# A GroupNorm, attention and 7x7 convolution kernel: edge rows stored once per column phase and read at offsets, constants kept in buffers, one block of v begun earlier

## The chip, the core and the metric

The kernel runs on one core of a Trainium2 chip, in one launch. The core has a matrix engine (TensorE, in the profile PE, its weight loads PEld), three engines for element-wise work (VectorE or DVE, ScalarE or ACT, GpSimd or POOL) and a queue that only issues transfers (SyncE, SP). Transfers between the chip's memory (HBM, tensors in a pool called `dram` here) and the on-chip buffers are issued by SP, ACT or POOL and carried by 16 DMA engines that all of them share. The metric is the device time of one execution in microseconds, lower is better.

## What is computed

Everything is float32. Two layers follow each other on an image `x` of 384 channels, 192 x 192:

```python
def layer0(x):                            # x: (1, 384, 192, 192)
    qkv = einsum('bchw,oc->bohw', x, w_qkv) + b_qkv           # 1152 channels
    qkv = qkv.reshape(b, 3*c, 96, 2, 96, 2).max(axis=(3, 5))  # 2x2 max pooling
    qkv = depthwise_conv3x3(qkv, w_dw) + b_dw
    q, k, v = split(qkv, 3)                                   # 8 heads of 48 channels
    q, k = q / norm(q), k / norm(k)                           # over the 9216 places
    attn = einsum('bhcn,bhdn->bhcd', q, k) * temperature      # 48 x 48 per head
    out = sum(topk_softmax(attn, kk) @ v * a for kk, a in ((24, a1), (32, a2), (36, a3), (38, a4)))
    out = repeat2x2(gelu(out))
    return einsum('bchw,oc->bohw', out, w_proj) + b_proj

def layer1(x):                            # depthwise 7x7, padding 3
    w_sym = (w + rot90(w, 1) + rot90(w, 2) + rot90(w, 3)) * 0.25
    return depthwise_conv7x7(x, w_sym)

x = x + layer0(groupnorm(x))              # 32 groups
x = x + layer1(groupnorm(x))
```

## The kernel before

Five stages follow each other.

**Statistics (0 to 130 us).** `x` is read once for the first GroupNorm.

**q and k (130 to 1330 us).** 24 blocks of eight image rows: TensorE multiplies (`pooled`, L662), VectorE pools and runs the 3x3 taps (`depthwise`, L717), transposes feed the products q times k in `grams`. Beside it, POOL builds the weights of the 7x7 convolution: `weights` (L571) writes banded weight rows into a tile `g` and stores them to two tensors in HBM, `wt` (inner rows) and `wh` (edge rows). SP stores a few constant rows from the tile `z` into `wh` and `sh` (L620 to L631).

**Attention's matrix (1330 to 1440 us).** `attention` (L881) is a generator: each `next` puts some of its steps into the program, and between them stand multiplications for v. It ends with a matrix `diag` filled by ten small transfers (L983), transposed on TensorE into `aT` (L990) and copied to `attnT`.

**v, projection, residual (1440 to 2190 us).** The image's rows are dealt into 16 blocks of two rows of each of six row bands of 32 (TR = 32, NT = 6, RB = 2), in the order 13, 14, 15, 0, 1, and so on. For each block i (L1217) `load_v` fills a third of the buffer `xvs` from SP's queue, `convolve` multiplies and pools, `depthwise_v` runs the taps, `attend` and `project` follow for block i - 2, and `residual` (L1142) adds the image rows `xr` (three buffers, loaded by SP, L1139) and stores the result for the last stage. Instructions marked `keep` stay in the written order on their engine.

`residual` writes a tile `sx` (three buffers in turn). The image's columns are split into four phases (CP = 4): column 4j + p is element j of phase p. A row of `sd` is one phase of one row in all six bands, RUN = 6 x 50 elements. Every block's two rows go to `sd` by POOL (L1197). The convolution of a band also needs three rows above and three below it. The first and the last three rows of the bands (block rows 0 to 2 and 29 to 31, that is blocks 14, 15, 0 and 1) are stored a second time, as edge rows, to `sh`, shifted by one band. Ten column shifts are wanted (NQ = CP + 7 - 1 = 10), so each edge row is stored three times, with four, four and two shifts (L1204 to L1210).

**The 7x7 convolution (2190 to 2775 us).** 48 steps of eight channels (CB = 8). The 128 partitions hold 4 phases x 32 rows. A step multiplies three weight tiles with three data tiles: two column offsets of `main` and one tile `aux` with all that `main` lacks. In `aux`, partitions 0 to 31 and 96 to 127 are copied from `main`; partitions 32 to 95 are read from `sh`: 30 upper edge rows, a row of ones (it carries the bias), a zero row, 30 lower edge rows, two zero rows. Loads run two steps ahead into three buffers each (`w`, `h`, `main`, `aux`), the first two steps' from SP, the others from ACT's queue (L1304). Per step, POOL runs `borders` for the next step (L1462): it adds the channel's mean, through masks in `mm`, to the padding columns of `main` and `aux`, and writes it by a copy into the padding rows of `aux`, so that padding becomes zero after the second GroupNorm. POOL also rearranges the result (`spread`, L1521), and SP stores it. VectorE puts 1/rstd into the middle of the weights (`middle`, L1405). The lines that read the edge rows:

```python
def load_aux(n):
    aux = auxs[n % len(auxs)]
    queue(n)(aux.rearrange("p c t j -> p c (t j)")[TOP:REST], sh[:, span(n)])
    return aux
```

Of the kernel before, what the change touches and what calls it, by code (L numbers as in the profile page):

```python
# [13 lines left out]
P = 128  # L14
# [55 lines left out]

TOP = 32
BOT = 64
ONE = TOP + HALO * NQ
# [13 lines left out]
def conv_preact_d2(  # L87
# [29 lines left out]
    sh = dram.tile([SHR, C, RUN], F32, name="sh")  # L117
# [445 lines left out]
    with ExitStack() as bx:  # L563
# [6 lines left out]
        def weights(kt, i0, i1):  # L570

            g = gwp.tile([P, GR, GQ, TR], F32, name=f"g{kt}_{i0}", tag="g")
            nc.gpsimd.memset(g, 0.0)
            for kr in range(KS):
                lo, hi = max(i0, kr), min(i1, kr + TR)  # L580
                if lo < hi:
                    nc.gpsimd.tensor_copy(
                        bass.AP(
                            g.tensor,
                            g.offset + ((lo - i0) * GQ + CP - 1) * TR + lo - kr,
                            [g.ap[0], [TR, KS], [GQ * TR + 1, hi - lo]],
                        ),
                        w7s[:, kt, kr, :].unsqueeze(2).to_broadcast([P, KS, hi - lo]),
                    )
            lo, hi = max(i0, HALO), min(i1, HALO + TR)  # L590
            cs = slice(kt * P, (kt + 1) * P)
            for v in range(CP if lo < hi else 0):
                nc.gpsimd.dma_start(
                    wt[v * TR + lo - HALO : v * TR + hi - HALO, cs].rearrange("f c n -> c f n"),
                    bass.AP(
                        g.tensor,
                        g.offset + ((lo - i0) * GQ + v) * TR,
                        [g.ap[0], [GQ * TR, hi - lo], [1, 2 * P]],
                    ),
                )  # L600
            for i in range(i0, i1):
                if HALO <= i < HALO + TR:
                    continue
                f = i * NQ if i < HALO else BOT - TOP + (i - HALO - TR) * NQ
                nc.gpsimd.dma_start(
                    wh[f : f + NQ, cs].rearrange("f c n -> c f n"),
                    bass.AP(
                        g.tensor,
                        g.offset + (i - i0) * GQ * TR,
                        [g.ap[0], [TR, NQ], [1, P]],  # L610
                    ),
                )
# [6 lines left out]
        with tc.issue_after(loaded):  # L619
            for kt in range(KT):  # L620
                cs = slice(kt * P, (kt + 1) * P)
                for f in (ONE, BOT + HALO * NQ):
                    nc.sync.dma_start(
                        wh[f - TOP : f - TOP + 2, cs].rearrange("f c n -> c f n"),
                        z[:, RUN : RUN + 2 * P].rearrange("p (f n) -> p f n", f=2),
                    )
                    for k in range(2):
                        one = f + k == ONE
                        nc.sync.dma_start(
                            sh[f + k - TOP, cs], z[:, 0:RUN] if one else z[:, RUN : 2 * RUN]  # L630
                        )  # L631
# [249 lines left out]
    def attention(ap):  # L881
# [102 lines left out]
        yield  # L984
        for dt in range(KT):
# [3 lines left out]
            for ct in range(lo // P, (hi - 1) // P + 1):  # L989
                nc.tensor.transpose(  # L990
                    ps[:, ct * P : (ct + 1) * P], diag[:, ct, dt * P : (dt + 1) * P], ident
                )
# [57 lines left out]
    with tc.tile_pool(name="ap", bufs=1) as ap:  # L1050
        chain = attention(ap)
        for _ in range(9):
            next(chain, None)
        i = AHEAD - 1
        for t0 in range(0, NT, UT):
            xb = load_v(i, t0)
            with tc.issue_after(multiplied):
                for ct in range(KT):
                    convolve(i, t0, ct, xb, lambda ins: ins)
            for _ in range(6):  # L1060
                next(chain, None)
        for ct in range(KT):
            depthwise_v(1, ct, (0, 1))
        for _ in chain:
            pass
# [76 lines left out]
    def residual(i, ot, y, xr, pin):  # L1142
# [52 lines left out]
        for a in range(RB):  # L1195
# [3 lines left out]
            halos = []  # L1199
            if r >= TR - HALO:  # L1200
                halos.append(((r - TR + HALO) * NQ, -JP))
            if r < HALO:
                halos.append((BOT - TOP + r * NQ, JP))
            for h, shift in halos:  # L1204
                for q in range(0, NQ, CP):
                    nv = min(CP, NQ - q)
                    nc.gpsimd.dma_start(
                        sh[h + q : h + q + nv, cs].rearrange("f c n -> c f n"),
                        rows_of(a, nv, shift + q // CP),
# [7 lines left out]
    for i in range(AHEAD, NBC):  # L1217
        j = i - 2
        xb = load_v(i, 0)
        for ct in range(KT):  # L1220
# [58 lines left out]
    with ExitStack() as ex_:  # L1279
# [57 lines left out]
        def load_aux(n):  # L1337
            aux = auxs[n % len(auxs)]
            queue(n)(aux.rearrange("p c t j -> p c (t j)")[TOP:REST], sh[:, span(n)])
            return aux  # L1340

# [3 lines left out]
        for n in range(2):  # L1345
            ws[n] = ws[n] if n == 0 else load_w(n), hs[n]
# [4 lines left out]
        mask = wide.tile([P, 5], F32, name="mask")  # L1351
# [4 lines left out]
        part = wide.tile([P, 4], F32, name="part")  # L1356
        for k, (base, q) in enumerate(((TOP, 0), (BOT, 0), (TOP, NQ - HALO), (BOT, NQ - HALO))):
            hits = ident[:, base : base + HALO * NQ].rearrange("p (h q) -> p h q", q=NQ)
            nc.vector.tensor_reduce(
                part[:, k : k + 1], hits[:, :, q : q + HALO], AX.XY, ALU.add  # L1360
            )
        nc.vector.tensor_tensor(mask[:, 3:4], part[:, 0:1], part[:, 1:2], ALU.add)
        nc.vector.tensor_tensor(mask[:, 4:5], part[:, 2:3], part[:, 3:4], ALU.add)
# [30 lines left out]
        mm = wide.tile([P, C, 5], F32, name="mm")  # L1394
# [30 lines left out]
        def masked(kt):  # L1425
            keep(
                nc.vector.tensor_tensor(
                    mm[:, tiled(kt), :],
                    mb[:, tiled(kt)].unsqueeze(2).to_broadcast([P, P, 5]),
                    mask.unsqueeze(1).to_broadcast([P, P, 5]),  # L1430
# [9 lines left out]
        masked(0)  # L1440
# [3 lines left out]
        middle(0)  # L1444
        sumw = const.tile([P, KT], F32, name="sumw")
# [14 lines left out]
        nc.sync.dma_start(wh[ONE - TOP].rearrange("(t p) n -> p t n", p=P), offs)  # L1460

        def borders(n):  # L1462
# [24 lines left out]
            for base, t in ((TOP, 0), (BOT, NT - 1)):  # L1487
                ends = aux[base : base + TOP, :, :, 0 : NJ : NJ - 1]
                keep(
                    nc.gpsimd.tensor_tensor(  # L1490
                        ends, ends,
                        mm[base : base + TOP, cs, 3:5].unsqueeze(2).to_broadcast([TOP, CB, NT, 2]),
                        ALU.add,
                    )
                )
                keep(
                    nc.gpsimd.tensor_copy(  # L1497
                        aux[base : base + HALO * NQ, :, t, 0:NJ],
                        mb[base : base + HALO * NQ, cs].unsqueeze(2).to_broadcast(
                            [HALO * NQ, CB, NJ]  # L1500
                        ),
                    )
                )
# [154 lines left out]
```

## Time and profile before

| what | us |
|---|---|
| median of 3 runs | 2758.66 |
| lowest and highest of them | 2756.45, 2759.91 |
| the profiled execution, whole | 2777.17 |
| its span in the profile | 2775.5 |
| TensorE busy in it | 2584.4 |
| VectorE busy | 2449.2 |
| ScalarE busy | 1141.4 |
| GpSimd busy | 744.6 |

The span is the time from the first to the last instruction of the one execution that was profiled. Busy times add up the instructions of an engine. Strips of 40 digits show the busy share of an engine in 40 equal slices of the span (69.4 us each), in tenths; PEclk is the clock granted to TensorE. In the lines on groups and waits, "L549 PE MATMUL pv<-xv,wq" is line 549, its engine and operation, the tile written and those read; "<-" at the end of a line names what an engine waited for. The share of DMA is the mean over 16 engines.

### The profile page before, as it was taken

The page shows a single profiled execution, that of the slowest core. Times are in us where ns is not written, and L with a number is a line of the kernel's source. Part 1 is how long each engine was busy: PE and PEld are TensorE (multiplying, and loading weights), DVE is VectorE, ACT ScalarE, POOL GpSimd, SP SyncE. Part 2 cuts the span into 40 slices and gives each one's busy share as a digit, 9 for nine tenths or more (in the row PEclk, how much of TensorE's full clock was granted, in tenths as well). Part 3 has the DMA queues.
Part 4 walks back from the last instruction along what each step waited for, and adds up shares of the span by engine and source line. Part 5 has one row for each costly group of instructions (what it writes and reads, how often), then busy time and mean ns, then how long its engine had stood idle before and what let it go on. Part 6 is the DMA issues. An engine that isn't in the chain of part 4 may idle for free. (4 is left out here: it accounts for less than half of the span.)

```text
span 2775.5 us, 25750 instructions
## 1 busy us (share of the span) xinstructions
PE 2584.4 (93%) x8365; PEld 1525.9 (55%) x8365; DVE 2449.2 (88%) x3538; ACT 1141.4 (41%) x2262; POOL 744.6 (27%) x885
## 2 busy tenths in 40 slices
PE   0399999999999999999979969999999899999998
PEld 0144444444444444444646646666666677777776
DVE  7989999999999999999889859989889788888887
ACT  0143333343433343443302212222324577777776
POOL 1024444100000000000011321010101578877876
PEclk9999999999999999999999989999999899999999
DMA  9976667311010101112227997575665899999998
GB/s 379 402 257 216 231 221 251 121 53 50 35 68 35 68 35 45 58 34 68 83 90 248 350 331 247 174 253 201 221 223 172 330 343 364 370 372 371 365 376 260
DMA packets 234087, 581.01 MB, mean 209 GB/s; under 512 B 16688, under 2 KB 165792, under 8 KB 217184
## 3 DMA queue, kind: packets, MB, share of 16 engines
q1 hardware_dynamic: 173456, 283.44, 29.2%
q0 software_dynamic: 37376, 148.85, 15.9%
q10 hardware_dynamic: 23120, 147.07, 14.1%
q8 instruction: 67, 1.10, 0.2%
q14 instruction: 68, 0.56, 0.1%
HBM read 370.93 MB, written 208.21 MB: 209 GB/s over the span
## 5 line engine op out<-in xcount | busy, mean ns | idle before, releaser
L662 PE MATMUL pq<-xq,wq 128*128 128x512 f32 x2268 | 1021.9, 595 | 0.0
L717 DVE SCALAR_TENSOR_TENSOR qk<-ring,wd,qk 128x384 f32<-128x384 f32 x1152 | 696.3, 615 | 25.0
L662 PEld LDWEIGHTS pq<-xq,wq 128*128 128x128 f32 x2268 | 411.7, 190 | 421.9 <-issue 371.4
L549 PE MATMUL pv<-xv,wq 128*128 128x384 f32 x1512 | 500.3, 491 | 29.2 <-DMA xv<-in_x_dram 23.9
L1562 PE MATMUL pc<-main,w 128*128 128x288 f32 x1536 | 435.2, 406 | 3.7 <-POOL aux L1497 1.1
L549 PEld LDWEIGHTS pv<-xv,wq 128*128 128x128 f32 x1512 | 289.1, 192 | 231.5 <-issue 22.6
L1582 DVE TENSOR_SCALAR apart<-pc,rb 32x576 f32<-32x576 f32 x384 | 312.2, 813 | 75.6 <-PE pc L1562 59.4
L1562 PEld LDWEIGHTS pc<-main,w 128*128 128x128 f32 x1536 | 289.3, 189 | 88.4 <-issue 3.4
L672 DVE TENSOR_REDUCE ring<-pq 128x128 f32<-128x512 f32 x428 | 290.0, 679 | 52.2 <-PE pq L662 51.4
L1580 ACT ACTIVATE apart<-pc,rb 32x576 f32<-32x576 f32 x384 | 281.4, 733 | 132.3 <-PE pc L1562 127.5
L735 ACT COPY qkT<-turns 32x288 f32<-32x288 f32 x768 | 329.5, 429 | 12.0 <-DVE turns L781 3.2
L1039 DVE SCALAR_TENSOR_TENSOR vb<-rows,wd,vb 128x576 f32<-128x576 f32 x384 | 313.2, 817 | 11.1
L729 ACT ACTIVATE junk<-qk 128x384 f32<-128x384 f32 x144 | 71.2, 494 | 471.9 <-DVE qk L717 471.1
L1562 PE MATMUL pc<-aux,h 128*128 128x288 f32 x768 | 248.5, 405 | 0.3 <-issue 0.3
L803 POOL TENSOR_TENSOR rn<-rn,halfpos 128x6 f32<-128x6 f32 x1 | 1.4, 1362 | 842.8 <-DVE rn L802 842.8
L1521 POOL COPY res<-apart 128x1152 f32<-128x1152 f32 (+1 forms) x96 | 223.4, 2353 | 10.8 <-ACT apart L1580 7.3
L1156 DVE TENSOR_TENSOR sx<-xr,y 128x576 f32<-128x576 f32 x180 | 203.8, 1174 | 24.0 <-ACT y L1127 14.9
L1197 POOL DMA_DIRECT2D sd<-sx x96 | 72.4, 757 | 517.2 <-DVE sx L1156 496.2
L555 DVE TENSOR_REDUCE rows<-pv 128x192 f32<-128x768 f32 x144 | 137.6, 956 | 71.8 <-PE pv L549 71.8
L1405 DVE SCALAR_TENSOR_TENSOR w<-eye,sb,w 128x512 f32<-128x512 f32 x96 | 171.9, 1830 | 1.5
L1176 ACT ACTIVATE wq<-sx,negmid 128x1152 f32<-128x1152 f32 x96 | 120.6, 1257 | 125.3 <-DVE sx L1156 121.2
L1562 PEld LDWEIGHTS pc<-aux,h 128*128 128x128 f32 x768 | 144.7, 189 | 42.8 <-POOL main L1470 1.9
(234 smaller groups left out, 2252.3 us busy)
## 6 DMA issues: line engine op xcount, KB each, us to landing
sd<-sx POOLq DMA_DIRECT2D x96, 600.0 KB, 10.3
out_dram<-res SPq DMA_DIRECT2D x192, 288.0 KB, 11.0
main<-sd ACTq DMA_DIRECT2D x46, 1200.0 KB, 6.9
xr<-in_x_dram SPq DMA_DIRECT2D x45, 1152.0 KB, 12.8
xq<-in_x_dram SPq DMA_DIRECT2D x21, 2304.0 KB, 7.9
xv<-in_x_dram SPq DMA_DIRECT2D x126, 384.0 KB, 7.0
w<-wt ACTq DMA_DIRECT2D x46, 1024.0 KB, 6.9
xs<-in_x_dram SPq DMA_DIRECT2D x24, 1536.0 KB, 15.1
```

Of the source, the lines that this page charges most:

```text
L549: nc.tensor.matmul(ps[:, u, 0 : RB * HW], wq[:, kt, o : o + P], xb[:, u, kt, :], start=(kt == 0), stop=(kt == KT - 1),)
L662: ins = nc.tensor.matmul(ps, wq[:, kt, ct * P : (ct + 1) * P], rows[:, kt, :, g * 64 : (g + 1) * 64], start=(kt == 0), stop=(kt == KT - 1) ...
L672: ins = nc.vector.tensor_reduce(t[:, r0 : r0 + PR, 1 + g * 32 : 1 + (g + 1) * 32], ps.rearrange("p (h a w b) -> p h w a b", h=PR, a=2, b=2 ...
L717: pin(nc.vector.scalar_tensor_tensor(dst, src, w, dst, ALU.mult, ALU.add))
L735: nc.scalar.copy(side[f * Q : (f + 1) * Q].rearrange("p c (t n) -> p t c n", n=P)[:, :, :, a * Q : (a + 1) * Q], turns[a * Q : (a + 1) * Q ...
L1039: pin(nc.vector.scalar_tensor_tensor(dst, src, w, dst, ALU.mult, ALU.add))
L1156: nc.vector.tensor_tensor(bass.AP(flat.tensor, flat.offset + at(e) + a * RUN, [flat.ap[0], [JP, NT], [1, NJ], [at(f) - at(e), 2]],), xq[:, ...
L1405: nc.vector.scalar_tensor_tensor(mid, eye.unsqueeze(1).to_broadcast([P, 4, P]), sb[:, c : c + 1], mid, ALU.mult, ALU.add,)
L1521: keep(copy(res[ps, k], apart[ps, :, k].rearrange("p e n -> p n e")))
L1562: nc.tensor.matmul(ahead[q][:, k, 0 : NT * NJ], lhs, rhs, start=(j == 0), stop=(j == 2), skip_group_check=True,)
L1580: keep(nc.scalar.mul(dst, src, scale))
L1582: keep(nc.vector.tensor_scalar_mul(dst, src, scale))
```

## The change

Edge rows. `sh` gets 24 rows (EDGE = 2 x 3 x 4: above and below, three rows, four phases) and one zero row. `residual` stores each edge row once, all four phases, 250 of 300 elements, without the shifts. `load_aux` reads 48 partitions with a pattern that walks offset 0 and then offset 1 over the 24 rows, and 12 more (two phases of each of six rows) at offset 2: two transfers a step in the place of one. `wh` gets the same order of rows, in up to three stores per edge row. Elements of `sh` that no store of `residual` fills are set to zero by SP from `z`.

Constants. The row of ones and the three zero rows go to a small tensor `cst`, and are loaded once into each of the three `aux` buffers, whose steps no longer overwrite them.

Padding rows. They now arrive as zeros, so `borders` adds the mean to them where it copied it before; the masks grow from 5 to 11 columns.

Attention. The generator's last part is held back: the loads, taps and multiplications of block 3's first third stand ahead of the transposes `aT`, which are now kept in order.

```diff
 TOP = 32
 BOT = 64
-ONE = TOP + HALO * NQ
+EDGE = 2 * HALO * CP
+ONE = TOP + 2 * HALO * NQ
 REST = 96
...
-    sh = dram.tile([SHR, C, RUN], F32, name="sh")
+    sh = dram.tile([EDGE + 1, C, RUN], F32, name="sh")
+    cst = dram.tile([REST - ONE, P, RUN], F32, name="cst")
...
-                f = i * NQ if i < HALO else BOT - TOP + (i - HALO - TR) * NQ
-                nc.gpsimd.dma_start(
-                    wh[f : f + NQ, cs].rearrange("f c n -> c f n"),
...
+                h = i if i < HALO else i - TR
+                for q in range(0, NQ, CP):
+                    nq = min(CP, NQ - q)
+                    f = q * 2 * HALO + h * nq
+                    nc.gpsimd.dma_start(
+                        wh[f : f + nq, cs].rearrange("f c n -> c f n"),
...
+            for k in range(REST - ONE):
+                nc.sync.dma_start(cst[k], z[:, 0:RUN] if k == 0 else z[:, RUN : 2 * RUN])
+
+            for kt in range(KT):
+                cs = slice(kt * P, (kt + 1) * P)
+                nc.sync.dma_start(sh[EDGE, cs], z[:, RUN : 2 * RUN])
+                for f in range(0, EDGE, EDGE // 4):
+                    o = 0 if f < EDGE // 2 else RUN - JP
                     nc.sync.dma_start(
+                        sh[f : f + EDGE // 4, cs, o : o + JP].rearrange("f c n -> c f n"),
+                        z[:, RUN : RUN + EDGE // 4 * JP].rearrange("p (f n) -> p f n", n=JP),
+                    )
...
-        for _ in range(9):
-            next(chain, None)
+        advance(9)
...
         for ct in range(KT):
             depthwise_v(1, ct, (0, 1))
+
+        advance(99)
+        xb = load_v(AHEAD, 0)
+        for ct in range(KT):
+            depthwise_v(AHEAD - 2, ct, (2,), keep)
+            convolve(AHEAD, 0, ct, xb, keep)
         for _ in chain:
             pass
...
-            halos = []
-            if r >= TR - HALO:
-                halos.append(((r - TR + HALO) * NQ, -JP))
-            if r < HALO:
-                halos.append((BOT - TOP + r * NQ, JP))
-            for h, shift in halos:
-                for q in range(0, NQ, CP):
-                    nv = min(CP, NQ - q)
+            for h, to, o in ((r - TR + HALO, JP, 0), (HALO + r, 0, JP)):
+                if h in range(HALO) if to else r < HALO:
                     nc.gpsimd.dma_start(
-                        sh[h + q : h + q + nv, cs].rearrange("f c n -> c f n"),
-                        rows_of(a, nv, shift + q // CP),
+                        sh[h * CP : (h + 1) * CP, cs, to : to + RUN - JP].rearrange(
+                            "f c n -> c f n"
+                        ),
+                        rows_of(a, CP, o)[:, :, 0 : RUN - JP],
                     )
...
-            queue(n)(aux.rearrange("p c t j -> p c (t j)")[TOP:REST], sh[:, span(n)])
+            flat = aux.rearrange("p c t j -> p c (t j)")
+            row = C * RUN
+            for p, q, rows in (
+                (EDGE * 2, 0, [[1, 2], [row, EDGE]]),
+                (2 * HALO * (NQ - 2 * CP), 2, [[CP * row, 2 * HALO], [row, NQ - 2 * CP]]),
+            ):
+
+                o = TOP + q * EDGE
+                queue(n)(
+                    flat[o : o + p],
+                    bass.AP(sh.tensor, sh.offset + n * CB * RUN + q, rows + [[1, CB * RUN]]),
+                )
             return aux
+
+        def load_constants(aux):
+            flat = aux.rearrange("p c t j -> p c (t j)")
+            keep(nc.sync.dma_start(flat[ONE:REST], cst[:, 0:CB]))
...
-        masked(0)
+        masked(0, 0, 3)
...
         middle(0)
+        masked(0, 3)
...
-            for base, t in ((TOP, 0), (BOT, NT - 1)):
-                ends = aux[base : base + TOP, :, :, 0 : NJ : NJ - 1]
-                keep(
-                    nc.gpsimd.tensor_tensor(
-                        ends, ends,
-                        mm[base : base + TOP, cs, 3:5].unsqueeze(2).to_broadcast([TOP, CB, NT, 2]),
-                        ALU.add,
-                    )
-                )
-                keep(
-                    nc.gpsimd.tensor_copy(
-                        aux[base : base + HALO * NQ, :, t, 0:NJ],
...
+            for base in (TOP, BOT):
+                ps = slice(base, base + TOP)
...
+                add(aux[ps, :, 1 : NT - 1, 0 : NJ : NJ - 1], 3, 5)
+                add(aux[ps, :, 0 : NT : NT - 1, 0:NJ], 5, 7)
+                add(aux[ps, :, 0 : NT : NT - 1, 0 : NJ : NJ - 1], 7, 11)
```

## The prediction

> **What bounds the kernel now.** I read the page first, then TensorE's waits, its timeline around the two longest late waits, the DMA view of the same stretch, and last the engines in the final stage.
>
> ```profile
> span 2775.5 us, 25750 instructions
> ...
> PE   0399999999999999999979969999999899999998
> ...
> PEclk9999999999999999999999989999999899999999
> DMA  9976667311010101112227997575665899999998
> ```
>
> TensorE (PE) is full nearly everywhere, so time is won only in its holes; the DMA engines are full in slices 22 to 24 (1457 to 1665 us) and again through the final stage, the last nine slices. TensorE's waits:
>
> ```profile
> PE pv L549 <- DMA xv<-in_x_dram: 23.9, 4, 18.2
> ...
> PE aT L990 <- DMA diag<-mix: 13.2, 1, 13.2
> ```
>
> The first is a transfer that came late, the second the end of attention's chain. The timeline of TensorE there (start, duration, line, count, idle before):
>
> ```profile
> 1566.27 8.89 PE L1119 MATMUL pr<-gl,wp 128*128 128x288 f32 x36
> 1575.00 13.06 PE L549 MATMUL pv<-xv,wq 128*128 128x384 f32 x40
> 1588.94 10.59 PE L549 MATMUL pv<-xv,wq 128*128 128x384 f32 x32 [0.89 <-DMA xv<-in_x_dram]
> ...
> 1643.88 1.62 PE L549 MATMUL pv<-xv,wq 128*128 128x384 f32 x2 [18.18 <-DMA xv<-in_x_dram]
> 1648.32 1.65 PE L549 MATMUL pv<-xv,wq 128*128 128x384 f32 x2 [2.83 <-DMA xv<-in_x_dram]
> 1651.97 25.22 PE L549 MATMUL pv<-xv,wq 128*128 128x384 f32 x68 [2.00 <-DMA xv<-in_x_dram]
> ```
>
> Blocks of v begin at 1449.85, 1499.46, 1548.84, 1599.37, 1677.03 and 1726.41 us (their first `po` matmul): 49.4 us each, but 50.5 and 77.7 in two. What fills the queues then, in the DMA view of 1470 to 1620 us:
>
> ```profile
> q0 software_dynamic: 7728, 32.54, 61.7%
> ...
> sh<-sx POOLq DMA_DIRECT2D x30, 600.0 KB, 16.9
> ```
>
> The edge rows `sh` (30 of 600 KB and 15 of 300 KB) are 23 of 50 MB there. The final stage, 2300 to 2700 us: first the row of the windows view (sum, PE, PEld, DVE, ACT, POOL busy; clock, DMA share, GB/s), then POOL's groups by shape:
>
> ```profile
> 2300.00:2700.00 400.00, 399.10 (x1639) 308.60 (x1638) 350.25 (x342) 305.96 (x374) 318.91 (x308) 1.00 1.02 370
> ...
> L1521 POOL COPY res<-apart 128x1152 f32<-128x1152 f32 x69 | 161.8, 2371 | 2.6 <-ACT apart L1580 0.5
> ...
> L1497 POOL COPY aux<-mb 30x384 f32<-30x384 f32 x69 | 34.4, 499 | 4.4
> L1490 POOL TENSOR_TENSOR aux<-aux,mm 32x96 f32<-32x96 f32 x68 | 29.6, 435 | 4.6
> L1470 POOL TENSOR_TENSOR main<-main,mm 128x96 f32<-128x96 f32 x34 | 13.4, 394 | 0.0
> L1470 POOL TENSOR_TENSOR main<-main,mm 128x48 f32<-128x48 f32 x34 | 10.4, 307 | 67.4 <-DMA main<-sd 55.3 <-PE pc L1562 12.1
> ```
>
> A step (eight channels, 48 matmuls) takes TensorE 11.65 us without a hole. But the DMA share is 1.02: the 16 engines have no room either, and POOL has 2.3 us.
>
> [...] The trace agrees so far: in its DMA records the 4-byte packets on SP's queue number 7552, which is 16 for each transfer but 8 for the two `h<-offs`, whose slowest counts are 8; on ACT's queue 3792 fit the same way. No wide transfer of before has a small slowest count. [...] the records show 361 ns for a 9600-byte packet (26.6 GB/s), at the tenth percentile as at the median: a ceiling per engine. [...] from L1470's rows the trace shows (394 - 307)/48 = 1.8 ns.
>
> **The change part by part.**
>
> *Edge rows stored once.* 54 `sh` transfers (27.6 MB) become 18 of 128 x 4 x 1000 bytes (9.2 MB), and 36 issues at 746 ns leave POOL's queue, behind which the `sd` stores wait; the buffers of `sx` come free sooner, then `xr`, and behind `xr` on SP's queue `xv`. A block without edges moves 10.8 MB in 49.4 us (216 GB/s); the two worst add 9.2 MB (405 GB/s, above the 360 seen at a full queue) and after the change 3.1 MB (280 GB/s). So the backlog doesn't form and the two long blocks fall to 49.4 us: (50.5 - 49.4) + (77.7 - 49.4) = 29.4 us gained, matmuls slowed after the hole included. If half the backlog stayed, 15.
>
> *v's fourth block ahead of `aT`.* TensorE idles 13.18 us before `aT`; 18 matmuls (6.0 us at 8.01 us for 24) move into it, and their three loads are issued at 1407 us already. But the third group needs a buffer that a reduction frees, and in the built order that reduction and two more 0.73-us taps stand ahead of the last `mix` on DVE: the chain, the `diag` transfers and `aT` end some 2.5 us later. Net 3.5 us (0 to 6).
>
> *The weights `wh` and the constants.* 18 issues of 972 ns become 54 of perhaps 750, 23 us more of POOL, at 170 to 560 us; SP's 18 small stores become 22, twelve of them in 200-byte pieces (9216 in all, 576 an engine, at 13 to 21 ns some 10 us), issued by 165 us, before SP stands waiting until 194 for a buffer. The matmuls of that stretch don't wait for DMA, and `wt` and `wh` are read at 2160 us. Nothing; without that cover, up to 10 us. The three loads of constants are four rows each: nothing.
>
> *Masks.* Some nine DVE instructions of 0.15 us beside the statistics, and the wide part of `mm` (1024 elements, about 1.2 us) behind `middle(0)`: the first borders end some 3 us later, once.
>
> *POOL's borders.* Per step two adds (0.44) and two copies (0.50) become six adds of 64, 768 and 32 elements: by 1.8 ns an element from 307 at 48, 0.34 + 1.60 + 0.28 = 2.22 us, twice. POOL's step goes from 9.4 to 9.4 - 1.9 + 4.4 = 11.9 us [...]: alone it would set the step at about 12.0.
>
> *Two transfers at offsets.* This decides. `load_aux` reads `sh` by a pattern whose outermost count is 2 (the offsets 0 and 1) over 24 rows, into 48 partitions: k is 2. The second is 6 over 2, into 12: k is 6. So engines 0 and 1 carry 24 + 2 rows of 9600 bytes a step where every engine carried 4. Engine 0's step, by the medians in the records: `w` 8 x 0.309, `h` 4 x 0.159, `main` 8 x 0.361, edge rows 26 x 0.361, marks 0.1, together 15.5 us; output 96 x 0.036 = 3.5 us. That is 19.0 us against TensorE's 11.65. Three buffers let two loads stand queued, so the engine stays fed and TensorE waits every step; POOL's 12 us and the late masks hide beneath. End: first load by ACT at 2199.4 us, 9 us of backlog from step 1's edge rows, 46 loads x 15.5 = 713, 44 outputs x 3.5 = 154: step 47's rows land at 3075 us. Then two borders' adds 4.5, the last step at a partly lowered clock 12.5, and the tail as before (2775.5 - 2761.5) 14: 3106. Less 29.4 + 3.5: a span of 3073, 298 over 2775.5. The profiled execution itself took 2777.17 us, 18.5 over the median 2758.66; I add the difference to the median: 3057, say **3055 us**.
>
> Bounds of the unknowns: if neighbouring packets overlap, as the share of 1.02 to 1.04 allows, 3% of 867 is 25 less; at mean instead of median durations (375, 392, 38.6 ns) it is some 65 more. Gains of 20 to 40. So 3000 to 3135.
>
> **The rivals.**
>
> *The rows are spread over all engines (8%).* If the pattern reaches the queue in another form and k is 16, each engine carries 4 rows at most, as before. Then POOL sets the step: 0.35 x 46 = 16 us lost, 3 at the masks, 33 gained: 2758.7 - 14 = 2745 us, faster. For it: a builder may regroup (xr's read is carried as 768 rows). Against: offsets 0 and 1 of one row can't be merged with the row step. The point of decision: with e engines an engine's step is 9.6 + 0.361 x (48/e + 2) us, at e = 8 12.5, and 46 x 0.85 = 39 us eats the gain of 33. So up to about eight engines the change is slower.
>
> *Two engines, but other ones each time (3%).* The mean load is then as before, the edge rows only land some 9 us after their issue, against a slack of about 7 us between the end of borders and the step that needs them: some 0.5 us a step, 2745 + 20 = 2765. For it: nothing[...].
>
> [...] All rows of engine 1 start 4 bytes off. At double time its step is 19.0 + 8.7 us and the end is 46 x 8.7 = 400 later: 3455 us. Against: no 9600-byte read of before lies so, but stores read `sx` at 4-byte shifts at 193 ns for 4800 bytes, close to the aligned rate.
>
> **How the numbers follow.** Two fixed engines bind: 85%, 3055 us, its own range 3000 to 3135 holding some 95% of it; the others 8, 3 and 4%. The range stays there, leaving two in ten out. What a measurement tells from no change is 0.2%, about 5 us. Slower: 85 + 4 + half of the rotating case, 90%; no change 2%; faster 8%.
>
> **What would show it.** Right: in the final stage steps of 18 to 20 us, TensorE at six tenths of busy, holes ended by the edge rows' transfers or POOL behind them, the mean DMA share at 0.6 to 0.7 while one transfer takes over 9 us to land; around 1600 us blocks of 49.4 us, no wait for `xv`; before `aT` a hole about 6 us shorter. Wrong: steps near 12 us with POOL full, a share near 1.0. The forecast fails wholly if the pattern is spread; it fails in size if packets on a lone engine overlap, or if the loads are issued too late to keep it fed.

## The result, and the profile after

| | median us | lowest and highest |
|---|---|---|
| before, 4 runs beside it | 2759.28 | 2756.45, 2765.2 |
| after, 4 runs | 3108.18 | 3107.46, 3109.22 |

The changed kernel takes 1.1253 times as long (95% interval 1.1232 to 1.1274): 349 us more. Its profiled execution has a span of 3106.9 us. From its page, the span, TensorE's strip, the granted clock and the DMA share:

```profile
span 3106.9 us, 25858 instructions
...
PE   0499999999999999999999999997777777777776
...
PEclk9999999999999999999999999998888888888888
DMA  9987765011010110132876657558666666666666
```

A slice is 77.7 us here. The dip of before near 1600 us is gone; TensorE stays at nine tenths until slice 27 and then stands at seven tenths to the end, while the DMA share, nine tenths there before, is six. So nothing shown as a mean is full. The row of the windows view for 2300 to 2700 us, in the columns used above:

```profile
2300.00:2700.00 400.00, 283.99 (x969) 210.03 (x968) 159.28 (x201) 187.28 (x229) 233.26 (x227) 0.85 0.69 222
```

TensorE 284 of 400 us where it had 399, POOL 233 where it had 319, 222 GB/s where 370 moved. All engines do the same work less often. The granted clock is 0.85 here, but that is not what makes a step long: 48 matmuls of 0.29 us (284 us by 969) are 14 us, and a step takes 19.5. The waits (engine, operation, line, what ended the wait: us in total, times, longest), TensorE's answer and then one line of all engines':

```profile
PE pc L1619 <- issue: 150.0, 29, 6.3
...
PE pc L1619 <- POOL main L1525: 90.0, 16, 6.8
...
PE pc L1619 <- DMA h<-offs: 10.5, 1, 10.5
```

```profile
POOL aux L1554 <- DMA aux<-sh: 279.9, 46, 8.7
```

POOL waits 46 times, once a step, for the edge rows, and TensorE waits for POOL behind it ("issue" stands where the profile does not show what ended a wait). POOL's groups by shape in the same 400 us show that the new additions are not what fills a step:

```profile
L1578 POOL COPY res<-apart 128x1152 f32<-128x1152 f32 x42 | 89.8, 2173 | 1.4 <-POOL aux L1554 0.2
L1554 POOL TENSOR_TENSOR aux<-aux,mm 32x768 f32<-32x768 f32 x41 | 61.2, 1493 | 0.0
...
L1554 POOL TENSOR_TENSOR aux<-aux,mm 32x64 f32<-32x64 f32 x40 | 17.4, 434 | 123.0 <-DMA aux<-sh 121.8
L1554 POOL TENSOR_TENSOR aux<-aux,mm 32x32 f32<-32x32 f32 x41 | 11.0, 269 | 3.2
```

The first of the three additions, 434 ns long, has 123 us of idle time ahead of it.

How few engines carry the edge rows can be counted in the trace's records of completion marks. Of the changed kernel's transfers in 48 steps, each load of `w`, `h` and `main` and each output store has 16 marks. The transfer of 48 rows has a single mark 1.08 to 1.60 us after its issue and then two, that of 12 rows one after 1.16 to 1.23 us and then six. The 4-byte packets agree: ACT's queue has 3424 of them here and 3792 before, 368 less, which is 46 loads of 8 marks (2 + 6) in the place of 16. The transfer of 48 rows issued at 2514.91 us has its two later marks at 2531.09 and 2531.53; that of 12 rows issued at 2515.61 has four by 2523.07 and two at 2532.16 and 2532.53. The output store issued at 2501.49 has 14 of its 16 marks by 2504.78 and the last two at 2512.73 and 2513.24. Read as one mark for each engine that carries a part, the early one apart, two engines run some 8 us behind the others; in each of 18 steps from 2300 to 2650 us the fifth of the six marks comes 8.5 to 9.7 us after the fourth, and the sixth 9.0 to 10.6. The records name no engine, so this reading is the author's. The packets of 2300 to 2700 us fit it: exactly two are in flight for 25% of the time, and fewer than two for 0.3%. By both, two engines are nearly always at work and the others often not.

Earlier in the program TensorE's timeline shows what the change gains (start, duration, idle before):

```profile
1432.89 6.80 PE L554 MATMUL pv<-xv,wq 128*128 128x384 f32 x12 [4.22 <-DVE rows L560]
1439.52 0.93 PE L1005 MATMUL aT<-ident,diag 128*128 128x128 f32 x7
...
1492.19 5.98 PE L1121 MATMUL po<-vb,attnT 128*128 128x288 f32 x24
...
1541.57 5.98 PE L1121 MATMUL po<-vb,attnT 128*128 128x288 f32 x24
...
1590.95 5.98 PE L1121 MATMUL po<-vb,attnT 128*128 128x288 f32 x24
...
1640.33 5.98 PE L1121 MATMUL po<-vb,attnT 128*128 128x288 f32 x24
```

`aT` has no idle time ahead of it any more (13.18 us before), and the blocks stand 49.38 us apart without a gap. TensorE begins the final stage at 2167.53 us, 31.2 us earlier than before (2198.72). So the change gains some 31 us up to there and loses some 360 in 48 steps.

### The profile page after: what moved, and what is told of

Read it like the earlier page. It is cut to its first block, busy times and chain, and to the rows that moved or that the text cites. A ratio compares the mean times of both kernels' runs of the same rounds, so it can differ in the third digit from the quotient of the medians.

```text
span 3106.9 us, 25858 instructions
## 1 busy us (share of the span) xinstructions
PE 2688.3 (87%) x8365; PEld 1588.8 (51%) x8365; DVE 2350.1 (76%) x3547; ACT 1140.7 (37%) x2262; POOL 841.7 (27%) x981
## 5 line engine op out<-in xcount | busy, mean ns | idle before, releaser
L1619 PE MATMUL pc<-aux,h 128*128 128x288 f32 x768 | 296.9, 473 | 253.6 <-issue 148.9
L1619 PE MATMUL pc<-main,w 128*128 128x288 f32 x1536 | 495.2, 450 | 2.0 <-issue 1.1
L1619 PEld LDWEIGHTS pc<-main,w 128*128 128x128 f32 x1536 | 331.0, 216 | 109.5 <-issue 2.3
L1619 PEld LDWEIGHTS pc<-aux,h 128*128 128x128 f32 x768 | 165.4, 222 | 319.2 <-issue 171.7
L1554 POOL TENSOR_TENSOR aux<-aux,mm 32x64 f32<-32x64 f32 (+2 forms) x288 | 207.3, 733 | 294.2 <-DMA aux<-sh 279.9
L1578 POOL COPY res<-apart 128x1152 f32<-128x1152 f32 (+1 forms) x96 | 208.0, 2203 | 6.5 <-DMA out_dram<-res 3.3
L765 PEld LDWEIGHTS grams<-qkT,qkT 128*96 128x96 f32 x576 | 92.3, 163 | 136.8 <-issue 132.1
```

The source lines that it names most:

```text
L1554: keep(nc.gpsimd.tensor_tensor(part, part, m, ALU.add))
L1578: keep(copy(res[ps, k], apart[ps, :, k].rearrange("p e n -> p n e")))
L1619: nc.tensor.matmul(ahead[q][:, k, 0 : NT * NJ], lhs, rhs, start=(j == 0), stop=(j == 2), skip_group_check=True,)
```

## The experiments

**One number for each kernel.** A step's length is taken from the trace as the mean interval between ACT's copies `h<-w 32x512`, one a step, from the third to the last but one of 48. The table has it beside two counts that the experiments turn: the edge rows on one engine, and the transfers that SP's and ACT's queues issue in a step. The rows are an estimate from the marks: each transfer's rows over its landing marks (without the single early one of a narrow transfer), summed over the step's transfers, as if these shared their engines. The landing marks are 16 for 64 rows in before, 16 and 16 for 48 and 16 rows in rows_48_16, 3 and 7 for 57 and 7 in rows_57_7, 2 and 6 for 48 and 12 in after and after_8, 2 and 2 for 62 and 2 in rows_62_2, 12, 12 and 6 for 24, 24 and 12 in after_split, and 12, 12 and 12 in by_shift; the kernels left have the reads of one of these.

| kernel | edge rows on one engine | transfers | step us | median us |
|---|---|---|---|---|
| before | 4 | 8 | 11.80 | 2759 to 2773 |
| rows_48_16 | 4 | 9 | 13.47 | 2848 |
| rows_57_7 | 20 | 9 | 17.34 | 3036 |
| after | 26 | 9 | 19.52 | 3108 |
| rows_62_2 | 32 | 9 | 21.44 | 3230 |
| after_8 | 26 | 8 | 21.11 | 3186 |
| after_split | 6 | 10 | 18.90 | 3070 |
| by_shift | 5 | 10 | 18.38 | 3045 |
| by_shift_act | 5 | 10 | 14.08 | 2846 |
| after_split_8 | 6 | 8 | 13.92 | 2849 |
| by_shift_act_8 | 5 | 8 | 13.18 | 2798 |
| copy_later | 4 | 8 | 11.77 | 2740 |

The theory on record is that two engines carry nearly all edge rows. The prediction and the expectations call the number of a transfer's engines k, and take for it the largest number up to 16 that divides the transfer's outermost counts. That rule of division was the author's assumption; the trace of before had one narrow case of it, `h<-offs`, with an outermost count of 8 and, beside an early one, eight marks, where the loads of the final stage have 16. The marks just listed agree with it in every transfer. The numbers that the engines are given there are names only. Against the theory stood the number of transfers, the unaligned offsets and POOL's additions.

### The kernel before, with only its read cut differently

```diff
-            queue(n)(aux.rearrange("p c t j -> p c (t j)")[TOP:REST], sh[:, span(n)])
+            flat = aux.rearrange("p c t j -> p c (t j)")[TOP:REST]
+            for lo, hi in ((0, 62), (62, 64)):
+                queue(n)(flat[lo:hi], sh[lo:hi, span(n)])
```

The two others have 48 and 57 in the place of 62.

> The kernel before, with one edit: the 64 aligned edge rows of a step are read by two transfers, of 62 and of 2 rows, in the place of one of 64. Few engines [...]: engines 0 and 1 carry 32 rows each; by 9.6 us of other packets and 0.361 to 0.38 us a row a step of 21.1 to 21.7 us, the end at 3190 to 3240 us. If instead the number of transfers a step, the reads at unaligned offsets or POOL's borders make the changed kernel slow: none of them but the first is here, and one transfer more costs at most a few us in all: 2755 to 2775 us.

> The kernel before, with the same 64 rows read by two transfers of 48 and 16 rows: as many transfers as in the 62 and 2 rows, but k = 16 for both, four rows an engine as with one transfer. Few engines: the time of before, 2755 to 2765 us. If the number of transfers costs: as slow as 62 and 2.

> The kernel before, with the same 64 rows read by two transfers of 57 and 7 rows: k = 3 and k = 7, so engines 0 to 2 carry 20 rows each. Few engines: a step of 9.6 + 20 x 0.361 = 16.8 us (17.2 at 0.38 us a row), 5.2 to 5.5 us over TensorE's 11.65 in some 46 steps: 2990 to 3015 us. This tells the rule of division from a simpler one, by which a small transfer is narrow and a large one always wide: by that one, 57 rows spread over 16 engines and the time stays at 2760 us. The number of transfers: as 62 and 2, as 48 and 16.

Measured against the kernel before: 62 and 2, 1.1656 (1.1637 to 1.1676), 3230.33 us; 48 and 16, 1.0274 (1.0257 to 1.0291), 2848.28 us; 57 and 7, 1.0951 (1.0933 to 1.097), 3036.05 us. The windows rows of 2300 to 2700 us, 48 and 16 first, then 62 and 2:

```profile
2300.00:2700.00 400.00, 363.31 (x1436) 275.42 (x1435) 293.12 (x301) 268.04 (x327) 280.69 (x268) 0.97 0.99 323
```

```profile
2300.00:2700.00 400.00, 253.28 (x891) 188.18 (x890) 152.12 (x188) 171.19 (x209) 172.73 (x171) 0.81 0.61 205
```

The same bytes, the same rows, two transfers in both: only the cut differs, and TensorE goes from 363 to 253 us, the DMA share from 0.99 to 0.61. So how the rows divide decides here, and the marks agree: 62 and 2 rows have two marks of landing each, 57 and 7 rows three and seven, 48 and 16 rows sixteen each. The first expectation holds; 57 and 7 is 21 us over its own, but far from the 2760 us of a wide transfer of 57 rows. With 20, 26 and 32 rows on an engine the steps are 17.34, 19.52 and 21.44 us: 0.34 us for each row between the first and the last. No unaligned read and no new addition is in these kernels. But 48 and 16 missed its expectation by 83 us: with 16 marks for each transfer a ninth one still costs 1.67 us a step. Two things differ there from before: packets of 9600 bytes take 449 ns in the mean where they took 372, at a DMA share of 0.99, and loads wait for stores, as the next section shows. Which of them costs how much was not taken apart.

### The changed kernel with its rows spread

```diff
-                (EDGE * 2, 0, [[1, 2], [row, EDGE]]),
+                (EDGE, 0, [[row, EDGE]]),
+                (EDGE, 1, [[row, EDGE]]),
```

> The changed kernel with one edit: the transfer whose outermost count is 2 (offsets 0 and 1 over 24 rows) becomes two transfers of 24 rows each, k = 12; the third keeps k = 6. At most six rows an engine in the place of 26: 9.6 + 6 x 0.37 = 11.8 us. Few engines: the final stage is then set by POOL or TensorE at about 12 us a step, and what the change gains elsewhere stays: 2735 to 2765 us. Reads at unaligned offsets (the same rows at the same offsets as in the changed kernel): stays at 3100 us. POOL's borders as the whole cause: stays at 3100 us. Three transfers a step in the place of two: no faster than the changed kernel.

3069.61 us, a ratio of 1.1068 (1.1051 to 1.1085): 38 us gained, not 350. The expectation failed, and by 300 us. The edit also makes ten transfers a step of nine, and the rival of three transfers in the place of two came closest. ACT's timeline of one step, 2502.8 to 2519 us (ACTq lines issue a transfer):

```profile
2502.83 0.35 ACTq L1330 DMA_DIRECT2D w<-wt  x1
...
2504.42 0.52 ACTq L1330 DMA_DIRECT2D aux<-sh  x1
...
2504.98 0.42 ACTq L1330 DMA_DIRECT2D aux<-sh  x1
...
2515.01 0.78 ACTq L1330 DMA_DIRECT2D aux<-sh  x1
2515.84 2.98 ACT L1638 ACTIVATE apart<-pc,rb 32x576 f32<-32x576 f32 x4 [9.68 <-PE pc L1620]
```

The third edge-row transfer is issued 10 us after the second, and the activations that clear TensorE's results stand behind it on ACT's queue; the profile puts their wait down to TensorE, but they start at 2515.84, when the issue is through (2515.79). What an issue waits for stands in the trace's records, not in the views: the record of a transfer has the number of the mark that it lands on and the number of one that it waits for. In before and in the changed kernel all transfers of SP and ACT land on eight numbers (100, 102 and 104 to 109); the changed kernel's `w` lands in successive steps on 104, 105, 106, 107, 108, 109, 100 and 102. Of their 272 and 185 issues from 2300 to 2700 us, 204 and 144 wait for the number that they will land on, and none of these starts before the transfer that had it last has landed; the others, `w` and a step's first store, show another number. A step of the changed kernel (us):

| transfer | issued | waits for | lands on | last landing on that mark before |
|---|---|---|---|---|
| first store | 2501.49 | 99 | 106 | |
| second store | 2501.85 | 109 | 109 | |
| third store | 2502.94 | 102 | 102 | |
| fourth store | 2503.85 | 105 | 105 | |
| `w` | 2513.31 | 110 | 106 | 2513.24, first store |
| `h` | 2513.68 | 108 | 108 | 2502.64, `main` of the step before |
| `main` | 2514.28 | 109 | 109 | 2513.92, second store |
| `aux`, 48 rows | 2514.91 | 102 | 102 | 2514.72, third store |
| `aux`, 12 rows | 2515.61 | 105 | 105 | 2515.51, fourth store |

The kernel before has eight transfers a step: its loads land on 104, 106, 107 and 109 every time, and each comes after the landing of the load one step ago. With ten, in after_split, a store and the step's last edge-row load have the same mark: the store issued at 2510.66 us and the load issued at 2515.01, and the store's last part lands at 2514.98. In 20 steps of 20 the load goes out 0.02 us (median) after such a landing. POOL's timeline of the same step:

```profile
2506.28 4.35 POOL L1579 COPY res<-apart 128x1152 f32<-128x1152 f32 x2 [4.04 <-ACT apart L1638]
```

The copies end at 2510.63, the store follows, the load is released at 2515.01, ACT clears the next results, and those the next copies wait for. By these records it is a closed ring of ACT, POOL, a store and ACT, 18.9 us long, in which nothing is full: for 20% of 2300 to 2700 us no packet at all is in flight, where before never has fewer than nine. With nine transfers loads are tied to stores too: in rows_48_16 the `w` load goes out within 0.25 us of the landing of a store with its mark in 28 steps of 30, in the changed kernel in 20 of 20.

### The same marks, taken out of the ring

```diff
-                    nc.sync.dma_start(
+                    (nc.gpsimd if q in (1, 3) else nc.sync).dma_start(
                         out[c : c + 2].rearrange("c (t r) w -> r (c t) w", t=NT),
```

In after_8 it is one of four stores (`(3,)`). POOL's transfers land on other marks, 111 to 118 in the records of before and of the changed kernel.

> after_split (three transfers of edge rows, k = 12, 12, 6; 3070 us) with two of the four output stores from POOL's queue, so eight transfers of SP and ACT a step in the place of ten. Shared marks as what held after_split at 18.9 us a step: both limits are gone, POOL's 11.5 and two issues of 0.75 leave 13.0 to 13.5 us, 2800 to 2835 us. Reads at unaligned offsets or POOL's borders as what held it: no gain, 3065 us or more.

> The changed kernel with one of a step's four output stores issued from POOL's queue in the place of SP's. [...] before has eight a step, the changed kernel nine, this one eight again. Nothing is altered in how edge rows spread over the engines. Few engines: engine 0 still carries 26 edge rows a step, 19.0 to 19.4 us a step, 3085 to 3110 us. The shared marks as the cause: steps of 12.3 to 13 us (POOL's 11.5 and one issue of 0.75), 2765 to 2810 us.

after_split_8: 2848.56 us, 1.0276 (1.0263 to 1.0289), 221 us less than after_split and 14 us over its range; no packet is in flight for only 3% of the time. Its windows row, and two of POOL's groups by shape there:

```profile
2300.00:2700.00 400.00, 353.30 (x1370) 265.62 (x1371) 238.87 (x285) 253.51 (x311) 378.52 (x371) 0.97 0.90 307
```

```profile
L1583 POOL DMA_DIRECT2D out_dram<-res x58 | 35.6, 618 | 9.5 <-POOL res L1579 8.6 <-DMA main<-sd 0.7 <-issue 0.2
...
L1526 POOL TENSOR_TENSOR main<-main,mm 128x96 f32<-128x96 f32 x28 | 19.4, 692 | 0.0
```

POOL is busy 378 of 400 us: now it is nearly full, and TensorE waits for it 29 times, once a step. A step is 13.92 us, 0.4 over the expectation; the additions to `main` take 692 ns here against 394 before. The reads are as unaligned as in the changed kernel, so offsets cost at most what is hidden under 13.9 us; in the changed kernel the median packet of 9600 bytes takes 361 ns, as before.

after_8: 3185.95 us, 1.1499 (1.1482 to 1.1517). Neither theory's number: 76 us over the one, 376 over the other. It rules out the marks as the sole cause, since eight transfers did not bring the time down: neither the marks alone nor, with ten transfers, the rows alone (after_split) win much, and after_split_8 has both edits. Its longest wait of POOL, and the stores in its DMA view (KB each, median us to landing):

```profile
POOL res L1578 <- DMA out_dram<-res: 162.0, 11, 20.4
```

```profile
out_dram<-res SPq DMA_DIRECT2D x57, 288.0 KB, 18.9
...
out_dram<-res POOLq DMA_DIRECT2D x19, 288.0 KB, 7.0
```

SP's stores land 18.9 us after their issue (11.2 in the kernel before), and POOL waits for their buffers. That the loads, no longer held back by the marks, queue ahead of these stores on the two engines would fit, and is not shown. The two engines are as full by the packets as in the changed kernel (fewer than two in flight for 1% of the time, 0.3% there), but packets of 9600 bytes take 433 ns in the mean, 379 there: by that, as an estimate, up to 1.8 us more for the 34 of a step on one engine, where the step is 1.6 us longer. Why they are slower stays open.

### Parts of the gain alone

attention_only gives the kernel before the reorder of attention. In stores_once each edge row is stored with its first four shifts only, so the convolution lacks the terms of the six others:

```diff
-                for q in range(0, NQ, CP):
+                for q in range(0, CP, CP):
```

> The kernel before with the change's reorder of attention alone (v's fourth block begun ahead of the transposes aT). By the prediction 3.5 us faster (0 to 6); by the two traces, in which the first po matmul comes 7 to 8 us earlier, up to 8 us faster. If the time is only shifted into the hole of v's later blocks: no change.

> The kernel before with each edge row stored to sh once, with its first four shifts only; the rows of the six other shifts are zeros that SP stores at the start, so these terms are left out of the convolution. The read, the borders and the steps are those of before. If the stores cause the hole of v's blocks: it is gone from the profile (blocks of 49.4 us), 29 us faster by the profile of before. If the execution without a profiler has less of the hole (the profiled one of before is 18.5 us over the median, that of after is level with it): 10 to 20 us faster. If the hole has another cause, such as SP's order of loads: no change.

attention_only: 0.9974 (0.9964 to 0.9983), some 7 us faster (5 to 10), nearer to the 8 us of the traces than to the prediction's 3.5. stores_once: 0.9913 (0.9895 to 0.9932), some 24 us faster (19 to 29), and in its trace blocks of v are 49.38 us apart and no wait for `xv` is left: the stores make the hole.

### Versions meant to keep the gain

by_shift reads rows in the order of the column shift (24, 24, 12 rows, k = 12), by_shift_act adds the second edit, by_shift_act_8 the two stores on POOL's queue as above.

```diff
-                (2 * HALO * (NQ - 2 * CP), 2, [[CP * row, 2 * HALO], [row, NQ - 2 * CP]]),
+                (2 * HALO * (NQ - 2 * CP), 2, [[row, 2 * HALO * (NQ - 2 * CP)]]),
...
-                spread(n - 1, last)
+                spread(n - 1, last, copies=[nc.gpsimd.tensor_copy, nc.scalar.copy])
```

> The changed kernel with the edge rows of a step in the order of the column shift: three transfers of 24, 24 and 12 rows, k = 12 each, so engines 0 to 11 carry five rows and the others none; the weight rows wh in the same order, one store per edge row, and simpler sums for the masks. Few engines: 9.6 + 5 x 0.37 = 11.4 us, below POOL's 11.5 to 12.0, so POOL sets the step: 2735 to 2755 us. If unaligned reads or a third transfer cost much: 2900 us or more.

> As by_shift, and one of the two copies of 1152 elements that rearrange a step's result goes from POOL to ACT. If POOL's borders bound by_shift: POOL has 9.4 us a step, TensorE's 11.65 us bind, 10 to 17 us faster than by_shift: 2720 to 2740 us, below both kernels. If not POOL but the DMA engines bound it: the same as by_shift.

> by_shift_act (2846 us) with two of the four output stores from POOL's queue: eight transfers of SP and ACT a step in the place of ten. POOL has 9.4 and 1.5, TensorE 11.65 us. Shared marks: steps of 11.7 to 12.2 us, 2735 to 2765 us, below the kernel before measured beside it, since what attention_only (7) and stores_once (25) gain is in it. DMA engines at their limit in place of the marks: 2830 us or more.

All three missed: 3044.87 us (1.0987, 1.0966 to 1.1008), 2846.29 us (1.0273, 1.0253 to 1.0294) and 2797.97 us (1.0093, 1.0077 to 1.011). by_shift has the ring of after_split: its third edge-row load is issued 9.4 us (median) after the second is through, and for 23% of 2300 to 2700 us no packet is in flight. So its number is that of the rival with a costly third transfer. Moving one copy gained 199 us where POOL's busy time would give 17: the copies are a link of the ring. With eight transfers the step is 13.18 us, not 11.65. Its windows row and POOL's longest wait there:

```profile
2300.00:2700.00 400.00, 368.14 (x1462) 280.55 (x1461) 259.76 (x304) 342.12 (x366) 329.89 (x365) 0.97 0.97 328
```

```profile
POOL main L1513 <- DMA main<-sd: 42.7, 26, 4.4
```

The DMA share is 0.97 at 328 GB/s, where before moves 370: full engines that move less. Packets of 9600 bytes take 425 ns in the mean, where they took 372. Four engines without edge rows (12 marks for each of its reads) do not explain it alone: rows_48_16 has 16 marks for each of its own, and 0.99 at 323 GB/s. The cause stays open.

So copy_later leaves the final stage alone. It is attention_only, with each edge row stored once in its block; the six other shifts are copied from `sh` to `sh` in blocks 6 to 11, where the DMA share of before is 0.65:

```diff
+        if LATER <= i < LATER + 2 * HALO:
+            k = i - LATER
+            h = k * NQ if k < HALO else BOT - TOP + (k - HALO) * NQ
+            for q in range(CP, NQ, CP):
+                nv, o = min(CP, NQ - q), q // CP
...
+                keep(nc.gpsimd.dma_start(part(h + q, 0), part(h, o)))
```

> The kernel before with the reorder of attention, and each edge row stored once (four shifts) in its block; the six other shifts' rows are filled by copies from sh to sh, 36 of 300 or 600 KB, issued from POOL's queue in blocks 6 to 11 of the v stage, where the DMA share is 0.65. The final stage, its read of 64 aligned rows in one transfer and its eight transfers a step are those of before. If the stores' timing and attention's order are all that the changed kernel gains: 25 + 7 = 32 us less the little that the copies take from the loads beside them, 25 to 32 us faster than the kernel before measured beside it, blocks of 49.4 us. If the copies hold up the loads of v or the stores of sd behind them: 0 to 20 us faster, with blocks longer than 49.4 us in blocks 6 to 11.

2740.25 us against 2763.53 beside it, 0.9919 (0.9897 to 0.9941): 22 us faster (16 to 28), just under the expectation. Three blocks in TensorE's timeline, the windows rows of 1700 to 2000 us (before first, then copy_later) and the copies in the DMA view:

```profile
1591.62 5.98 PE L1108 MATMUL po<-vb,attnT 128*128 128x288 f32 x24
1641.00 5.98 PE L1108 MATMUL po<-vb,attnT 128*128 128x288 f32 x24
1690.38 5.98 PE L1108 MATMUL po<-vb,attnT 128*128 128x288 f32 x24
```

```profile
1700.00:2000.00 300.00, 300.00 (x1024) 194.37 (x1023) 268.25 (x304) 85.31 (x185) 27.63 (x37) 1.00 0.65 216
```

```profile
1700.00:2000.00 300.00, 300.00 (x1021) 193.71 (x1020) 268.14 (x306) 82.67 (x180) 53.40 (x72) 1.00 0.84 268
```

```profile
sh<-sh POOLq DMA_DIRECT2D x18, 600.0 KB, 17.7
sh<-sh POOLq DMA_DIRECT2D x18, 300.0 KB, 17.7
```

Blocks of 49.38 us, TensorE full, a share of 0.84: the traffic was moved to where there was room, and the step of the final stage is 11.77 us. This version is faster than both kernels.

## Why the prediction held, and where it did not

The direction and the range held, and so did most signs that it named: a DMA share of 0.69, edge rows that land 16 us after their issue, blocks of 49.4 us. TensorE is busy at seven tenths and not six: a matmul takes 293 ns in the mean at the granted clock of 0.85 (284 us by 969), and took 244 at 1.00 (399 by 1639). One reading was loose: the DMA strip of before has seven tenths in slice 22, and is full in 23 and 24 only. By its own steps:

**Edge rows stored once: 29.4 us.** Right by the profile: the blocks are 49.38 us. In the medians stores_once alone gives 24 us.

**v's fourth block: 3.5 us.** Mis-sized. The term counted 18 matmuls into the gap; 36 moved, of which 24 follow on without a wait and 12 after 4.22 us. With 0.74 and 1.05 us at `attnT`, 6.0 us of the 13.18 are left, and attention_only gains some 7.

**Weights and constants: nothing; masks: 3 us once.** Not run alone. The earlier start by 31.2 us leaves room for no more than a few us. A term that the sum lacked follows it: 10.5 us for `h<-offs`, once, issued at 2165.53 us and waited for until 2182.10. That edge rows stand ahead of it on the full engines would fit, and is not shown.

**POOL's additions: 2.22 us, twice a step.** Right: 0.434 + 1.493 + 0.269 = 2.20.

**Two engines: 19.0 us a step.** The mechanism fits what was measured: the transfer of 48 rows has two landing marks, exactly two packets are in flight for 25% of the time, and the cut of the read alone moves the step from 13.47 to 21.44 us. The size was 0.5 us low, 24 us over 46 steps. The medians of packets were used; in the records of the final stage 9600-byte packets have a median of 361 ns but a mean of 379, and 34 of them on one engine make 0.6 us.

**The transfer to the median.** The sum gave a span of 3073, 34 us under the 3106.9: 24 from the steps, 10.5 from `h<-offs`, less some 4 at attention, and a rest of 3. The prediction then added its difference to the median, which carried the 18.5 us by which the profiled execution of before lay above its median; that of after lies level. These two make the 53 us between 3055 and 3108. Executions of before beside the experiments took 2750 to 2777 us, so the profiled one, at 2777.17, stands at the upper end of a wide spread. Where the 18.5 us lie was not settled.

**The rival of rows spread over all engines, 2745 us.** This failed. It held that POOL would set the step at 12.0 us and that the change pays from about eight engines up. With reads of twelve, twelve and six landing marks after_split takes 3070 us. The step that was missing: the prediction named what waits behind an issue on POOL's queue, but held two transfers in the place of one to be free on ACT's. The order in which loads and stores wait for each other is a limit of its own: the records show eight marks, and with the eight transfers a step of before each load has one to itself. So the number was right for a cause that the marks and the cuts of the read bear out, two engines. The ring of 18.9 us came with the tenth transfer. The changed kernel, with nine, has loads that wait for stores as well, but its two engines do not run dry meanwhile (fewer than two packets in flight for 0.3% of the time), so in its 19.52 us that wait costs little or nothing. What nine transfers would take with the rows of the changed kernel spread, no run shows. And with both limits lifted after_split_8 still takes 2849 us, 104 over the rival's number: POOL, with two stores to issue and slower additions, has no room left.

**Unaligned reads, 3455 us; other engines each time, 2765 us.** Both fell: the first by after_split_8, the second by steps that grow with the rows on one engine, and by the marks of the changed kernel's second transfer: two of its six come 8.5 to 10.6 us late, as they would on engines that carry the first as well.

## What to carry to other kernels

Read the outermost counts of both patterns of every transfer in a loop and count its landing marks: 48 rows read as 2 times 24 had two here, and 24 rows twelve. A mean DMA share of 0.6 to 0.7 with every step waiting for one transfer can be a few full engines (0.69 in the changed kernel, 0.61 in rows_62_2). It can also be a ring: after_split has 0.74. The number of packets in flight tells them apart here: in the changed kernel it is exactly two for a quarter of the time and fewer for 0.3%; in after_split it is none for a fifth of the time. Count the transfers of a step as well, and look in the trace's records for the mark that each waits for: in after_split a tenth transfer tied a load to a store of the same step, and the profile put 9.68 us of ACT's wait down to TensorE. When a saving in traffic is wanted, look first for a stretch with room to move it to.

## What the runs showed beside that

An edit that lifts one limit can bring another: taking the edge rows from 26 to 6 on an engine, at the price of a tenth transfer, gained 38 us, and going back to eight transfers gained a further 221. Copies from HBM to HBM, 16 MB in 36 transfers, cost TensorE nothing while the share rose from 0.65 to 0.84. An addition of 128 x 96 on POOL took 394 ns in one kernel and 692 in another; what slows it stays open.
